# Loads of x blocks 4 to 7 and of the feed-forward weights: from ScalarE's queue to SyncE's, behind a store that waits for block 2

## The chip, the cores and the metric

The kernel runs on one core of a Trainium2 chip. A core has five engines with a queue of instructions each: TensorE (PE, matrix products; its weight loads are listed apart as PEld), VectorE (DVE), ScalarE (ACT), GpSimd (POOL) and SyncE (SP), which here only issues transfers. Transfers run on 16 DMA engines that all queues share. The metric is device time in microseconds of one execution; less is better. Times quoted are the median of three runs, beside which one execution was profiled.

## The reference

The input x has 4 batches of 1024 tokens with 256 features. Four layers follow one another, each with a residual and with a layer norm in front:

```python
x = x + _L0_attn_a_ref(_layernorm(x), ...)   # linear recurrent unit (LRU)
x = x + _L0_ffn_ref(_layernorm(x), ...)      # feed-forward with two top-k gates
x = x + _L0_attn_b_ref(_layernorm(x), ...)   # attention, 8 heads of 64
x = x + _L0_ffn_ref(_layernorm(x), ...)      # the same feed-forward weights again
```

The LRU computes, for each batch, a complex linear recurrence over the tokens, and from its states the output:

```python
u = einsum('btd,edh->ebth', x, W_in) + b_in          # real, imaginary, direct
h[t] = lam * h[t-1] + gamma * (u[0] + i u[1])
out = h.real @ W_mid[0] - h.imag @ W_mid[1] + u[2]   # and b_mid
y = gelu(out @ w1_w + w1_b) @ w2_w + w2_b + out
y = layernorm(y) * ln_g + ln_b
```

The feed-forward layer makes logits by a grouped projection, a batch norm over all 4096 tokens (this is why it needs all blocks before it can go on), a gelu and a product with `lin_w`. It keeps the 32 largest of 256 softmax values on the output side and on the input side, and multiplies with one 256 x 256 weight.

## The kernel before

**Blocks.** x lies in eight SBUF tiles `blocks[0]` to `blocks[7]` of 512 tokens (512 KB each). Block k belongs to batch k // 2; the two blocks of a batch hold its even and its odd tokens (`by_block`), so that one recurrence with 512 steps serves both. Each tile has its own place, so none of the x loads waits for space.

**The LRU stage** (up to about 293 us) works block by block:
- `lru.head(xb[k])` (line 357) normalizes a block: DVE takes the statistics (L133, L134) and the inverse root (L55 to L66, L136), ACT scales (L145, `xn`), PE transposes (L147), ACT rounds the result to `xnt[k][0]` (L160) and DVE forms the remainder `xnt[k][1]` (L161). The transposed blocks have four buffers.
- `lru.states` (line 381) makes the states of one batch for one half c of the features: PE products `pu` (L170), evacuated by ACT into `u` (L390), then the recurrence on DVE (L402 to L416). `lru.evacuated` collects the ACT instructions of L390: numbers 0 to 3 belong to batch 0, 4 to 7 to batch 1.
- `lru.outputs` (line 422) is the way from the states to the new x of a block: PE `po` (L170, L437), ACT `ot` (L438), PE `pz` (L443), ACT gelu `zt` (L446), PE (L452), DVE (L455), PE transposes `py` (L465), statistics on DVE, ACT `yn` (L474), POOL (L482 to L484).

`tile_kernel` writes them down in this order: heads of blocks 0 and 1, states of batch 0, `output_weights`, heads of blocks 2 and 3, states of batch 1; then a loop over k with `lru.outputs` of block k, states of a later batch, `lru.head` of block k + 4, and from k = 2 on `f1.head` of block k - 2, which begins the first feed-forward layer. `f1.head` stores transposed inputs with SP (`tt`, L527).

**Loads.** SP loads blocks 0 and 1 at the start. ACT's queue loads the LRU's weights at the start, blocks 2 and 3 after the first `xnt` cast, `brow` (the gain and base rows) after `evacuated[3]`, and then, after `evacuated[7]`, blocks 4 to 7 and all of `ffn_weights` (line 995): the weight `w.wf`, the logits' weight `lint` in four pieces, and nine rows of 1 KB for the biases. The rows come in three groups: each group clears a tile `v` of a single buffer on POOL (L1028), loads one row into three partitions (L1030), and splits it into three bf16 parts by ACT casts (L1031, L1034, L1036) and POOL subtractions (L1032, L1035). The products that read `lint`, `linb` and `wf` are in the feed-forward layers, from 293 us on.

**What sets the order.** A planner orders each engine's instructions when the program is built, by their place in the source and by its own estimate of when their inputs are there; afterwards an engine takes its instructions strictly in that order, and each waits for what it needs. `with tc.issue_after(ins):` puts the instructions that the block writes on the engine of `ins` behind `ins` in that engine's order; it puts no order on other engines. In `with tc.issue_after(lru.evacuated[7])` it holds ACT's DMA issues and ACT's casts.

Of the kernel before, what the change touches and what calls it, by code (L numbers as in the profile page):

```python
# [10 lines left out]
F32 = mybir.dt.float32  # L11
# [10 lines left out]
P = 128  # L22
B = 4
T = 1024
D = 256
# [3 lines left out]
NBLK = B * T // 512  # L29
# [143 lines left out]
def by_block(v):  # L173

    return [
        v[b * T : (b + 1) * T, :].rearrange("(q p r) d -> r p q d", p=P, r=CH)[r] for b in range(B) for r in range(CH)
    ]
# [807 lines left out]
def run(*gens):  # L985
    for g in gens:
        for _ in g:
            pass
# [6 lines left out]
def ffn_weights(nc, rp, cp, w, lint, lin_t, w_ffn, rows):  # L995
    vecs = w.vecs


    grp = cp.tile([P, 32], F32, tag="grp", name="grp")
    nc.gpsimd.memset(grp, 1.0)  # L1000
    nc.gpsimd.affine_select(
        out=grp, in_=grp, compare_op=ALU.is_ge, fill=0.0, base=0, pattern=[[-4, 32]], channel_multiplier=1
    )
    nc.gpsimd.affine_select(
        out=grp, in_=grp, compare_op=ALU.is_ge, fill=0.0, base=3, pattern=[[4, 32]], channel_multiplier=-1
    )
    for s in range(2):
        for k in range(KD):
            nc.gpsimd.tensor_scalar(
                w.cw[:, k, s * 32 : (s + 1) * 32],  # L1010
                grp,
                vecs[:, V_CW + 2 * s + k : V_CW + 2 * s + k + 1],
                0.0,
                ALU.mult,
                ALU.add,
            )
    nc.gpsimd.memset(lint, 0.0)
    for s in range(2):
        for k in range(KD):
            r = k * 64 + s * 32  # L1020
            nc.scalar.dma_start(lint[r : r + 32, s, :], lin_t[s, k * 32 : (k + 1) * 32, :])
    nc.scalar.dma_start(w.wf, w_ffn)

    nc.gpsimd.memset(w.ones, 1.0)
    parts = [slice(32 * i, 32 * i + 32) for i in range(3)]
    for dst, at in ((w.linb[:, 0:D], 0), (w.linb[:, D : 2 * D], D), (w.bias, 4 * D)):
        v = rp.tile([P, D], F32, tag="v", name="v")
        nc.gpsimd.memset(v, 0.0)  # L1028
        for i in range(3):
            nc.scalar.dma_start(v[32 * i : 32 * i + 1, :], rows[0:1, at : at + D])  # L1030
        nc.scalar.copy(dst, v)  # L1031
        nc.gpsimd.tensor_tensor(v, v, dst, ALU.subtract)  # L1032
        for i in (1, 2):
            nc.scalar.copy(dst[parts[i], :], v[parts[i], :])  # L1034
        nc.gpsimd.tensor_tensor(v[parts[2], :], v[parts[2], :], dst[parts[2], :], ALU.subtract)  # L1035
        nc.scalar.copy(dst[parts[2], :], v[parts[2], :])  # L1036
# [3 lines left out]
def tile_kernel(ctx: ExitStack, tc: tile.TileContext, x_in, w_lru, vecs_in, rows, w_ffn, lin_t, w_attn, w_down, out):  # L1040
    nc = tc.nc
# [9 lines left out]
    def load_x(engine, blk):  # L1051
        engine.dma_start(blocks[blk], by_block(x_in)[blk])
# [9 lines left out]
    w = Weights()  # L1062
    w.ident, w.vecs = ident, vecs
    w.wf = cp.tile([P, KD, D], F32, tag="wf", name="wf")
    lint = cp.tile([P, 2, D], F32, tag="lint", name="lint")
# [5 lines left out]
    f1 = Ffn("f1", tc, bp, x, w)  # L1071
# [3 lines left out]
    with ExitStack() as c1:  # L1075
        psum = Banks(c1.enter_context(tc.tile_pool(name="ps1", space=PSUM)), {"pu": 2, "po": 2, "py": 2, "pt": 2})

        brow = c1.enter_context(tc.tile_pool(name="brow", bufs=1)).tile([P, 2, D], F32, tag="brow", name="brow")
        lru = Lru(tc, c1, ident, vecs, brow, w_lru, psum)
        xb = [x[4 * k : 4 * k + 4] for k in range(NBLK)]  # L1080
        xnt = [lru.head(xb[0])]
        lru.tables(lambda: xnt.append(lru.head(xb[1])))
        with tc.issue_after(lru.xnt_first):
            for blk in range(2, 4):
                load_x(nc.scalar, blk)
        h = [[lru.states(xnt, c) for c in range(KD)]]
        lru.output_weights()
        with tc.issue_after(lru.evacuated[3]):
            nc.scalar.dma_start(brow.rearrange("p a b -> p (a b)"), rows[0, 2 * D : 4 * D].partition_broadcast(P))
        xnt += [lru.head(xb[k]) for k in (2, 3)]  # L1090
        h.append([lru.states(xnt[2:4], c) for c in range(KD)])
        for k in range(NBLK):
            last = k >= NBLK - 2
            if k == 0:
                with tc.issue_after(lru.evacuated[7]):
                    for blk in range(4, NBLK):
                        load_x(nc.scalar, blk)
                    ffn_weights(
                        nc, c1.enter_context(tc.tile_pool(name="rows", bufs=1)), cp, w, lint, lin_t, w_ffn, rows
                    )  # L1100
            if k < NBLK - 1:
                run(lru.outputs(k % CH, xb[k], xnt[k], h[k // CH], (0, 1), last))

            b = k // CH + 1
            if 2 <= b < B:
                if k % CH == 0:
                    h.append([])
                h[b].append(lru.states(xnt[b * CH : (b + 1) * CH], k % CH))
            if k + 4 < NBLK:
                xnt.append(lru.head(xb[k + 4]))  # L1110
            if 2 <= k < NBLK - 2:
                run(f1.head(k - 2, lru.sp, psum, "pt"))
        for blk in range(4, NBLK - 3):
            run(f1.head(blk, lru.sp, psum, "pt"))
        k = NBLK - 1
        ot, zt = lru.buffers()
        halves = [
            lru.outputs(k % CH, xb[k], xnt[k], h[k // CH], (i,), last, tag, [v[:, :, c : c + 256] for v in (ot, zt)])
            for i, tag, c in ((0, "pu", 0), (1, "po", 256))
        ]  # L1120
        for i in (0, 0, 1):
            next(halves[i])
        run(f1.head(NBLK - 3, lru.sp, psum, "pt"))
        for i in (0, 1, 0, 1, 0, 1, 1):
            next(halves[i])
        with tc.issue_after(lru.last_gelu):
            run(f1.head(NBLK - 2, lru.sp, psum, "pt"))
        run(*(f1.head(NBLK - 1, lru.sp, psum, "pu", (i,), "lx", "zt") for i in range(2)))

    with ExitStack() as c2:  # L1130
# [7 lines left out]
        at = Attention(tc, x, ident, ident64, wqk, wvo, wd, sp, wp)  # L1138
        with ExitStack() as c4:
# [14 lines left out]
            first = at.prepare(0, 0, psum, "at")  # L1154
# [170 lines left out]
```

## Time and profile before

| | us |
|---|---|
| median of 3 runs | 1529.46 (1526.32 to 1533.48) |
| profiled execution, its own time | 1528.76 |
| profiled execution, span | 1527.0 |
| busy PE, DVE, ACT, POOL | 1286.5, 1184.6, 1017.5, 680.3 |

All times in the profile count from the start of the span. The timelines give the start and the length of instructions in order of time, those of one kind that follow one another merged (x4 means four of them); an engine's name with a q, such as ACTq, is its queue issuing a transfer. In brackets stands how long the engine sat idle before the instruction, and whose end let it go. The lists of waits give the total, the number and the longest. The LRU stage fills the first fifth of the span, the first feed-forward layer follows until about 390 us, attention with the second layer's heads between until about 1310, and the rest is the second feed-forward layer.

Over the span the page has 96.51 MB moved, a mean of 63 GB/s.

### The profile page before, as it was taken

To read this page: it belongs to the slowest core of one execution; us is meant where nothing else is said; L and a number is where in the kernel's file an instruction comes from. 1 tells how busy PE (TensorE), PEld (TensorE's weight loads), DVE (VectorE), ACT (ScalarE), POOL (GpSimd) and SP (SyncE) were. 2 spreads that over 40 slices of the span, in tenths; PEclk is the share of its full clock that TensorE was granted. 3 is DMA by queue.
4 is the path that set the end of the run, shared out by engine and by line. 5 is a ranking of instruction groups with operands and counts; after the bars stand their busy time and mean duration, and the time that the engine had idled before them with its cause. 6 is when DMAs were issued, how large, how long until landed. Compare 5 with 4: busy or idle time off the path is not lost. (4 is left out here: it accounts for less than half of the span.)

```text
span 1527.0 us, 28727 instructions
## 1 busy us (share of the span) xinstructions
PE 1286.5 (84%) x10134; PEld 955.6 (63%) x10136; DVE 1184.6 (78%) x3682; ACT 1017.5 (67%) x2152; POOL 680.3 (45%) x849
## 2 busy tenths in 40 slices
PE   4879998697898898888998989889999999566675
PEld 3535465376677766766776767677777777334454
DVE  8976665697868887878768687777676675599998
ACT  5353433566887877797777787877777776475674
POOL 2033332161545454544544554454344444067776
PEclk9999999698999999999999999999999999688899
DMA  3110000321454343434433445334344545000000
GB/s 118 32 41 15 21 21 21 128 97 49 84 93 90 61 77 73 77 70 82 82 74 60 72 79 86 61 61 83 68 82 79 92 86 96 1 15 24 22 25 28
DMA packets 288609, 96.51 MB, mean 63 GB/s; under 512 B 268233, under 2 KB 284626, under 8 KB 288466
## 3 DMA queue, kind: packets, MB, share of 16 engines
q1 hardware_dynamic: 283024, 88.50, 28.7%
q10 hardware_dynamic: 5442, 6.18, 1.2%
q8 instruction: 80, 1.31, 0.4%
q14 instruction: 63, 0.52, 0.1%
HBM read 16.01 MB, written 11.53 MB: 18 GB/s over the span
## 5 line engine op out<-in xcount | busy, mean ns | idle before, releaser
L898 POOL TENSOR_TENSOR pd<-pr,pd 128x1024 f16<-128x1024 f32 x128 | 273.5, 2141 | 247.6 <-ACT pd L897 185.7
L890 DVE TENSOR_REDUCE nm<-sc 128x1 f32<-128x1024 f32 x256 | 308.5, 1217 | 78.9 <-PE sc L886 77.5
L894 ACT ACTIVATE pr<-sc,nm 128x1024 f32<-128x1024 f32 x256 | 285.9, 1119 | 84.6 <-DVE nm L892 47.0
L886 PE MATMUL sc<-kh,qs 128*128 128x512 f32 x512 | 184.3, 438 | 26.4 <-ACT pr L894 18.8
L886 PE MATMUL sc<-kl,qs 128*128 128x512 f32 x512 | 162.0, 397 | 0.0
L674 DVE MATCH_REPLACE8 wk<-m,wk 128x256 f32<-128x256 f32 x384 | 154.9, 406 | 0.1
L910 ACT COPY p<-ptp 128x512 f32<-128x512 f32 x224 | 124.1, 590 | 45.3 <-PE ptp L905 33.7
L674 DVE MAX8 m<-wk 128x8 f32<-128x256 f32 x384 | 151.3, 412 | 0.4
L930 PE MATMUL pmo<-p,la 128*64 128x128 f32 x2048 | 144.0, 289 | 6.1 <-ACT ft L524 2.9
L905 PE MATMUL ptp<-ident,pr 128*128 128x128 f32 x1024 | 138.3, 275 | 12.9 <-ACT pr L894 12.4
L930 PEld LDWEIGHTS pmo<-p,la 128*64 128x64 f32 x2048 | 122.8, 144 | 25.0 <-ACT ft L524 5.1
L905 PEld LDWEIGHTS ptp<-ident,pr 128*128 128x128 f32 x1024 | 115.6, 140 | 34.8 <-ACT pr L894 22.2
L897 ACT CAST pd<-pr 128x1024 f16<-128x1024 f32 x128 | 133.5, 1054 | 5.6 <-DMA d<-pd 4.6
L886 PEld LDWEIGHTS sc<-kh,qs 128*128 128x128 f32 x512 | 85.2, 195 | 51.1 <-ACT pr L894 29.8
L886 PEld LDWEIGHTS sc<-kl,qs 128*128 128x128 f32 x512 | 97.0, 190 | 23.2 <-issue 1.4
L930 PE MATMUL pmo<-d,lb 128*64 128x128 f16 x3072 | 103.4, 222 | 7.6 <-DVE qs L853 2.6
L930 PEld LDWEIGHTS <-lb 128*64 128x64 f16 x3072 | 92.2, 111 | 26.3 <-issue 20.1
L628 POOL TENSOR_TENSOR ex<-ex,wk 128x512 f32<-128x512 f32 x61 | 77.6, 1273 | 57.4 <-DVE wk L674 45.5
L926 POOL COPY rows<-rs 128x128 f32<-128x128 f32 x128 | 36.1, 294 | 124.4 <-PE pmo L938 76.3
L941 DVE TENSOR_TENSOR on<-pmo,rb 128x128 f32<-128x128 f32 x128 | 36.4, 285 | 66.8 <-ACT rb L940 66.3
L147 PE MATMUL pt<-ident,xn 128*128 128x128 f32 x256 | 47.8, 309 | 44.5 <-ACT xn L145 32.9
L699 PE MATMUL pf<-wf,vt 128*128 128x256 f32 x288 | 81.2, 427 | 4.6 <-ACT vt L697 4.2
(307 smaller groups left out, 2768.6 us busy)
## 6 DMA issues: line engine op xcount, KB each, us to landing
tt<-ft SPq DMA_DIRECT2D x16, 256.0 KB
tt<-tt SPq DMA_DIRECT2D x8, 512.0 KB
out<-x SPq DMA_DIRECT2D x32, 128.0 KB
x<-in_x ACTq DMA_DIRECT2D x6, 512.0 KB
pf<-pfs SPq DMA_DIRECT2D x12, 256.0 KB
full<-pf SPq DMA_DIRECT2D x24, 128.0 KB
d<-pd SPq DMA_TRANSPOSE x128
wa<-in_w_attn SPq DMA_DIRECT2D x2, 640.0 KB
```

Source lines behind the costliest of these rows:

```text
L147: nc.tensor.transpose(pt[:, k, i * P : (i + 1) * P], xn[:, k * P : (k + 1) * P], ident)
L628: pool.tensor_tensor(ex, ex, wk, ALU.subtract)
L674: ins = make(*args).ins
L699: nc.tensor.matmul(dst, vt[:, k, :], w.wf[:, k, :], start=(k == 0 and bias is None), stop=(k == KD - 1))
L886: nc.tensor.matmul(sc[:, sl], qs[:, j, q * P : (q + 1) * P], kk[:, sl], start=(i == 0), stop=(i == 1))
L890: nc.vector.tensor_reduce(nm, sc, AX.X, ALU.max, negate=True)
L894: nc.scalar.activation(pr, sc, AF.Exp, bias=nm, accum_out=ssum[:, j : j + 1])
L897: nc.scalar.copy(pd[:, 0, :], pr)
L898: nc.gpsimd.tensor_tensor(pd[:, 1, :], pr, pd[:, 0, :], ALU.subtract)
L905: nc.tensor.transpose(pt[:, kk, :], pr[:, kc * P : (kc + 1) * P], self.ident)
L910: nc.scalar.copy(dst, pt)
L930: nc.tensor.matmul(po[j * HD : (j + 1) * HD, 0, :], v, pts[j][:, c, :], start=(n == 0), stop=(n == len(terms) - 1),)
```

## The change

Two things change. The loads of `lint`, `wf` and the nine `v` rows are issued by SP in place of ACT, and so are the loads of blocks 4 to 7. And their place in the order is given by a new instruction: SP stores one column of `xnt[2][0]` (128 partitions, 4 bytes each) to a scratch tile `gate` in DRAM, which nothing reads; the loads stand behind it on SP. The store waits for the data that it reads, which ACT's cast writes in the head of block 2; the loads behind it wait with it. In the source the x loads now stand ahead of the states of batch 1, and `ffn_weights` stays where it was.

```diff
@@ ffn_weights
-            nc.scalar.dma_start(lint[r : r + 32, s, :], lin_t[s, k * 32 : (k + 1) * 32, :])
-    nc.scalar.dma_start(w.wf, w_ffn)
+            nc.sync.dma_start(lint[r : r + 32, s, :], lin_t[s, k * 32 : (k + 1) * 32, :])
+    nc.sync.dma_start(w.wf, w_ffn)
...
-            nc.scalar.dma_start(v[32 * i : 32 * i + 1, :], rows[0:1, at : at + D])
+            nc.sync.dma_start(v[32 * i : 32 * i + 1, :], rows[0:1, at : at + D])
@@ tile_kernel
         xnt += [lru.head(xb[k]) for k in (2, 3)]
+        gate = f1.dram.tile([P, 1], F32, tag="gate", name="gate")
+        first = nc.sync.dma_start(gate, xnt[2][0][:, 0, 0:1].bitcast(F32)).ins
+        with tc.issue_after(first):
+            for blk in range(4, NBLK):
+                load_x(nc.sync, blk)
         h.append([lru.states(xnt[2:4], c) for c in range(KD)])
         for k in range(NBLK):
             last = k >= NBLK - 2
             if k == 0:
-                with tc.issue_after(lru.evacuated[7]):
-                    for blk in range(4, NBLK):
-                        load_x(nc.scalar, blk)
+                with tc.issue_after(first):
                     ffn_weights(
                         nc, c1.enter_context(tc.tile_pool(name="rows", bufs=1)), cp, w, lint, lin_t, w_ffn, rows
                     )
```

## The prediction

> **What bounds the kernel now.** I read the waits of each engine first, cut to the first 400 us, because every moved instruction lies there; then the timelines of ScalarE (ACT) and TensorE (PE) around the moved loads; then windows of 1 us, and wider ones after them, to see who is the limit before and behind that place. The longest waits that touch a moved load are one of ACT and, behind it, one of PE:
>
> ```profile
> ACT ot L438 <- DMA wf<-in_w_ffn: 9.2, 1, 9.2
> PE pz L443 <- ACT ot L438: 8.2, 1, 8.2
> ```
>
> The timeline of ACT shows what the 9.2 us are (start, length, engine, line, what):
>
> ```profile
> 72.19 0.78 ACT L390 ACTIVATE u<-pu,gb,par_o 128x512 f32<-128x512 f32 x1 [2.02 <-DVE h L402]
> 72.20 2.05 ACTq L1052 DMA_DIRECT2D x<-in_x  x4
> 74.29 2.02 ACTq L1021 DMA_DIRECT2D lint<-in_lin_t  x4
> 76.35 0.43 ACTq L1022 DMA_DIRECT2D wf<-in_w_ffn  x1
> 77.16 4.96 ACTq L1030 DMA_DIRECT2D v<-in_rows  x3
> 82.17 1.26 ACT L438 ACTIVATE ot<-po,ob 128x512 f32<-128x512 f32 x2 [9.20 <-DMA wf<-in_w_ffn]
> ...
> 87.25 0.84 ACTq L1030 DMA_DIRECT2D v<-in_rows  x3
> 88.12 1.28 ACT L446 ACT_TABLE_LOAD   x1 [1.28 <-DMA v<-in_rows]
> ```
>
> And that of PE, what stood behind it:
>
> ```profile
> 72.00 2.74 PE L437 MATMUL po<-h,wm 128*128 128x512 f32 x6
> 82.91 5.17 PE L443 MATMUL pz<-ot,w_lru 128*128 128x512 f32 x8 [8.18 <-ACT ot L438]
> 90.15 3.70 PE L452 MATMUL pz<-zt,w_lru 128*128 128x512 f32 x8 [2.08 <-ACT zt L446]
> ...
> 105.11 1.88 PE L443 MATMUL pz<-ot,w_lru 128*128 128x512 f32 x4
> ```
>
> The reader is to see that `po` of block 0 was finished at 74.74 and that ACT could not evacuate it before 82.17, because twelve DMA issues stood ahead of it in its queue. Three windows tell who is the limit (width, then busy us of PE, PE's weight loads, DVE, ACT, POOL; PE clock, DMA share, GB/s):
>
> ```profile
> 40.00:60.00 20.00, 15.75 (x67) 11.93 (x66) 20.00 (x33) 7.37 (x14) 0.00 (x0) 0.91 0.05 13
> 79.00:80.00 1.00, 0.00 (x0) 0.00 (x0) 1.00 (x5) 0.00 (x0) 0.00 (x0) 0.54 1.09 383
> 130.00:160.00 30.00, 29.36 (x107) 16.50 (x105) 22.08 (x59) 13.40 (x25) 13.18 (x22) 1.00 0.05 18
> 160.00:200.00 40.00, 36.99 (x133) 21.83 (x134) 25.27 (x76) 15.99 (x29) 16.36 (x24) 0.96 0.08 27
> ```
>
> VectorE (DVE) is never idle from 20 to 90 us; from about 95 to 240 us PE is the limit (92 to 98% busy). The stall lies at the joint: PE has work for blocks 0 and 1 at 75 us that needs no further states, and loses 8 us. So microseconds given to PE at 75 should survive: PE is short of time until 240, the stage behind it (240 to 290) is a chain of dependent steps, and the feed-forward layer cannot start its batch norm before all blocks are through.
>
> **What is removed.** ACT loses 4 x loads (2.05 us), 4 `lint` loads (2.02), `wf` (0.43) and nine `v` rows. The first three `v` take until 82.12: the second starts at 79.9 and the third at 81.9, though one issue lasts 0.23 to 0.47. Meanwhile the DMA engines are full (share 1.00 to 1.09 in most microseconds from 74 to 81), so the queue held the issuer back. The sum on PE:
> - The gap of 8.18. Without the DMAs, ACT evacuates `po` at 74.8; one evacuation (0.7 us) of the second half stays in the way: gain 7.5.
> - The clock. In the gap PE's granted clock falls to 0.54 and stays at 0.50 until 85; the eight L443 took 5.17 where four take 1.88 later, so 3.76: gain 1.4.
> - The second gap of 2.08: the activation table (1.28) is loaded at 88.12, behind casts and three more issues (0.84). The first half of `pz` would be finished 1.9 us after L443 starts, and table plus activation (1.28 + 0.63) then lie beside the other half: gain 1.8.
> - The third group of issues (0.84 at 94.4) delayed an `xnt` cast by 0.6, with PE busy: nothing.
> Together 10.7 us.
>
> Here a rule speaks against so much. The Trainium skill, "DMA: Bandwidth & Descriptors", section "Issuing engines are not separate DMA queues", says that choosing another issuing engine saves only the time to initiate a DMA, usually small beside the transfer, since all share the same 16 engines. By the rule only the issues count: 2.05 + 2.02 + 0.43 + 0.47 + 2 x 0.23 = 5.4 us from 72.97, so ACT would have been free at 78.4 and PE loses only 78.4 - 74.7 = 3.7; with the second gap that makes 5.5. The row says free at 82.17. I take the row: the issuer is blocked by the full queue as well, and after the change nothing urgent stands behind it. The bandwidth, as the rule has it, does not improve.
>
> **What is added and moved.** SP gets one store of 128 x 4 bytes. It waits for the `xnt` cast of block 2: 40.87 + 0.58 = 41.45 for its first half, or 47.7 if the whole tile counts. Behind it on SP come the 18 loads, in order; then nothing until the first `tt` store at 134.38. SP was empty from 2 to 134 us, so issue time there costs nothing. No row shows a store so small; bounds are 0 and the 3.5 us that x4 needed from issue (72.2) to first use (75.75). Nobody waits for its landing and x is not needed before 75: 0.
>
> The transfers, 2.5 MB, took from 73 to 81.6 and would run from 42 to 51 (or 48 to 57). The DMA share is 0.00 from 40 to 46; then only `brow` runs, first read at 105. Cost 0.
>
> The nine casts on ACT (0.40 each, 3.6 us) and POOL's three memsets and six subtractions come earlier. A group took 5.8 to 7.2 us from its first cast to that of the next (83.33, 90.57, 96.39), so three end about 72. ACT has idle stretches of 7.57, 1.78 and 6.31 us between 52 and 69, POOL is empty there: cover exists. Without cover, a cast that stands in ACT's queue ahead of its landing holds the `u` evacuations; DVE reaches block 2's `u` at 61.77, and it was ready at 60.5, so only 1.3 us of slack. POOL also disturbs DVE: beside POOL's subtraction at 83.80 DVE's L56 took 0.63 instead of 0.16. Six subtractions of 0.66 to 0.94 are 4.3 us, so this costs between 0 and 4.3; I take 1, as DVE's large operations (0.66 to 0.68) were not lengthened beside it.
>
> x4 to x7 in place by 51: their layer norms need about 18 us of DVE, now at 75 to 116 us. Done earlier in small holes they would help: a PE gap of 3.03 at 113.65 waited for DVE's L455, behind block 7's statistics. Put ahead of the state recurrences they would hurt. Bounds -3 and +18; I take 0, as both `lru.states` calls are written before those heads.
>
> **Sum**: -10.7 + 1 = -9.7. The profiled execution took 1528.76 us (span 1527.0 and 1.8 around it), which gives 1519; the median of the three runs is 1529.46, which gives 1520. I say 1520.0.
>
> **Rivals.**
> - *The wait moves to the casts.* The queue orders are fixed beforehand by a planner's own estimate of landings. If it places the first `linb` cast before block 3's `xn` at 46.67, ACT waits for the row behind 2.5 MB, until 51.5: 5 us, of which 1.3 is slack; with all of POOL's 4.3 on DVE it gives back 8. Result -10.7 + 8, about 1527. For it: DVE has no slack there. Against it: after 15 us ACT's only waits for a landing in this trace are of 0.8 us or less, apart from the queue's hold above.
> - *DVE's order turns.* With x4 to x7 early, the statistics (16 of 0.40, 16 of 0.15, and four inverse roots of a dozen operations each, 0.15 to 0.65) slip into the recurrences of batches 0 and 1. PE's L437 at 62.1 needs those states. Up to 18 us pushed ahead of it, less the 9.7: 1538. It decides once more than 9.7 us of statistics stand before the last L415 (61.17) on DVE. For it: DVE is the limit there, and 8 of those 18 us lay between the recurrences already at 75 to 90. Against it: their data order puts them behind, and the norm's buffers are double only.
> - *The change doesn't act*: `po` is not evacuated at 74.8 because something else stands ahead (the `linb` casts of group 3, or the planner puts L438 elsewhere): 0, about 1529. Small, as the DMAs are gone from ACT in any case; I count it with the first rival.
>
> **Chances.** Forecast 0.52 (own range 1514 to 1525); casts or no effect 0.23 (1523 to 1532); DVE's order, or another queue order that costs, 0.25 (1533 to 1545). A measurement of this kernel tells about 0.5% (7.6 us; the three runs lie 7.2 apart) from no change. Of the forecast's 0.52, 0.42 lies below 1521.8; the rest and the first rival make 0.33; slower is 0.25. The range 1513 to 1540 leaves out the fast end and the far part of the last case.
>
> **What would show it.** Right: on ACT no DMA issue after 20 us but `brow`; L438 within 1 us of the end of L437 near 75; PE's clock stays at 1.0 from 74 to 86; L446's table load directly behind L443's first half; the end of the LRU stage (293.4, first `wf` cast) about 10 us earlier. Wrong: an ACT wait for `v` between 45 and 70; layer-norm statistics of x4 to x7 before 61 on DVE and L437 later than 62; or the 10 us gained at 90 gone by 290, which would mean that PE was not the limit between.

## The result: slower by 0.6%, and the profile after

The changed kernel takes 1538.29 us (median of 9 runs, 1530.63 to 1545.40), the kernel before in the same comparison 1528.68 (9 runs, 1524.52 to 1533.48): ratio 1.0062, 95% interval 1.0037 to 1.0086. The forecast was 1520. The profiled execution after has a span of 1535.6 us.

I read the waits of the first 400 us first, as before (total, number, longest). In the kernel after they show two new waits, both for x, and the pair of waits at `ot` and `pz` is no longer among the longest:

```profile
DVE lx_st L133 <- DMA x<-in_x: 12.8, 3, 7.3
...
ACT xnt L160 <- DMA x<-in_x: 7.4, 1, 7.4
...
ACT linb L1031 <- DMA v<-in_rows: 5.0, 2, 2.8
```

The timelines of the same kernel, of SP, DVE, ACT and PE in turn, give the place:

```profile
41.84 0.34 SPq L1093 DMA_DIRECT2D gate<-xnt  x1
42.23 2.07 SPq L1052 DMA_DIRECT2D x<-in_x  x4
44.41 9.42 SPq L1021 DMA_DIRECT2D lint<-in_lin_t  x4
55.67 0.35 SPq L1022 DMA_DIRECT2D wf<-in_w_ffn  x1
...
45.63 1.22 DVE L410 TENSOR_TENSOR_SCAN h<-rad,h 128x512 f32<-128x512 f32 x1
54.17 1.08 DVE L133 BATCH_NORM_STATS2 lx_st<-x 128x6 f32<-128x256 f32 x3 [7.32 <-DMA x<-in_x]
...
54.17 0.35 ACTq L1089 DMA_DIRECT2D brow<-in_rows  x1
54.55 0.59 ACT L160 CAST xnt<-pt 128x512 fp32r<-128x512 f32 x1 [7.43 <-DMA x<-in_x]
...
82.48 0.69 ACT L438 ACTIVATE ot<-po,ob 128x512 f32<-128x512 f32 x1 [0.94 <-PE po L437]
...
71.54 3.60 PE L437 MATMUL po<-h,wm 128*128 128x512 f32 x8
84.00 3.60 PE L443 MATMUL pz<-ot,w_lru 128*128 128x512 f32 x8
```

The store is issued at 41.84 and the four x loads right behind it, as foreseen. But block 4 lands only at about 54, 12 us after its issue. The planner has put block 4's statistics (L133) right behind the first recurrence of batch 0 (L410) on DVE, the engine that this stage waits for, and DVE stands still for 7.3 us. In the kernel before, these statistics came behind batch 0's states, and `po` earlier (timelines of DVE and PE):

```profile
75.75 1.08 DVE L133 BATCH_NORM_STATS2 lx_st<-x 128x6 f32<-128x256 f32 x3
...
62.11 4.45 PE L437 MATMUL po<-h,wm 128*128 128x512 f32 x10
```

ACT stands too: the issue of `brow` (L1089) is released by the same landing, and the `xnt` cast of block 3 is queued behind it. PE's `po` products start at 71.54 where they started at 62.11, and `ot` comes at 82.48, no earlier than before (82.17), though no DMA issue stands in its way any more.

Windows of 1 us of the kernel after, and the 20 us that were shown of before (columns as there), tell why x was late:

```profile
43.00:44.00 1.00, 1.00 (x6) 0.82 (x5) 1.00 (x3) 0.39 (x1) 0.00 (x0) 1.00 0.25 49
44.00:45.00 1.00, 1.00 (x6) 0.77 (x6) 1.00 (x2) 0.39 (x1) 0.00 (x0) 1.00 0.00 0
...
47.00:48.00 1.00, 1.00 (x7) 0.82 (x6) 0.00 (x0) 0.12 (x1) 0.00 (x0) 1.00 0.42 22
...
50.00:51.00 1.00, 0.00 (x0) 0.00 (x0) 0.00 (x0) 0.00 (x0) 0.00 (x0) 1.00 0.52 27
...
52.00:53.00 1.00, 0.00 (x0) 0.00 (x0) 0.00 (x0) 0.00 (x0) 0.00 (x0) 1.00 0.96 311
...
40.00:60.00 20.00, 11.35 (x53) 8.72 (x54) 12.68 (x27) 7.02 (x13) 0.00 (x0) 0.86 0.59 137
```

Between 44 and 52 the queue moves 0 to 100 GB/s, with 2 MB of loads issued; then it runs at 311 GB/s and more. DVE, 20.00 of 20 us busy before, is busy for 12.68.

What became of the loss, from the same points in both profiles (us; the last column is `g_pitch`, the kernel with the spread-out store, explained below):

| point | before | after | after, spread store |
|---|---|---|---|
| imaginary part of batch 0's states finished (DVE L416) | 61.25 | 74.99 | 67.81 |
| real part finished (DVE L415); now all of them are there | 61.85 | 77.44 | 70.25 |
| first `ot` (ACT L438) | 82.17 | 82.48 | 76.14 |
| last step of the first batch norm (DVE L548, end of the LRU stage) | 296.82 | 299.31 | 287.79 |
| first row maximum of attention (DVE L890) | 378.15 | 384.18 | 372.93 |
| last step of the second batch norm (DVE L548) | 1325.13 | 1334.36 | 1325.96 |
| span | 1527.0 | 1535.6 | 1527.2 |

15.6 us are lost at batch 0's states (13.7 at the imaginary part, which is the point that the expectations below give). By the end of the stage 13 of them are made good; the stall at 75 is gone. Then 3.5 more are lost before attention, and the remaining 3.2 to the second batch norm.

### The profile page after: what moved, and what is told of

Its sections match the earlier page's. It is cut to its first block, busy times and chain, and to the rows that moved or that the text cites. A ratio compares the mean times of both kernels' runs of the same rounds, so it can differ in the third digit from the quotient of the medians.

```text
span 1535.6 us, 28749 instructions
## 1 busy us (share of the span) xinstructions
PE 1296.9 (84%) x10136; PEld 960.9 (63%) x10136; DVE 1179.1 (77%) x3682; ACT 1019.4 (66%) x2152; POOL 684.7 (45%) x849
## 5 line engine op out<-in xcount | busy, mean ns | idle before, releaser
L890 DVE TENSOR_REDUCE nm<-sc 128x1 f32<-128x1024 f32 x256 | 308.9, 1219 | 82.4 <-PE sc L886 81.0
L894 ACT ACTIVATE pr<-sc,nm 128x1024 f32<-128x1024 f32 x256 | 286.1, 1120 | 82.9 <-DVE nm L892 47.9
L674 DVE MATCH_REPLACE8 wk<-m,wk 128x256 f32<-128x256 f32 x384 | 160.7, 426 | 0.1
L674 DVE MAX8 m<-wk 128x8 f32<-128x256 f32 x384 | 155.5, 431 | 0.4
```

The costliest lines, as they stand in the source:

```text
L674: ins = make(*args).ins
L890: nc.vector.tensor_reduce(nm, sc, AX.X, ALU.max, negate=True)
L894: nc.scalar.activation(pr, sc, AF.Exp, bias=nm, accum_out=ssum[:, j : j + 1])
```

## Experiments

Theory A: the 128 four-byte writes of the store hold up the loads behind them in the queue, and x comes late for DVE. Theory B: the early place of the loads costs, by the planner's order (statistics of x4 to x7 and `v` casts ahead of the recurrences), or by transfers beside the work. All edits are made to the changed kernel.

**A wide store** (`wide`): 512 bytes for each partition in place of 4. Every queue has the same order.

```diff
-        gate = f1.dram.tile([P, 1], F32, tag="gate", name="gate")
-        first = nc.sync.dma_start(gate, xnt[2][0][:, 0, 0:1].bitcast(F32)).ins
+        gate = f1.dram.tile([P, P], F32, tag="gate", name="gate")
+        first = nc.sync.dma_start(gate, xnt[2][0][:, 0, 0:P].bitcast(F32)).ins
```

> The store ahead of the loads writes rows of 512 bytes (128 x 128 values) instead of 4 bytes; every engine's order of instructions is that of the changed kernel. Theory A (x4's data came 8 us late because they crept behind 128 writes of 4 bytes): the transfers of x4 to x7 start at about 43 and run at 300 GB/s or more, DVE's wait of 7.3 us for x4 and ACT's of 7.4 us shrink below 2, the states of batch 0 end near 68 instead of 75, and the time falls by 4 to 8 us, to 1530 to 1534. Rival B (the loads are slow there for another reason, or the wait is off the path): the wait stays at about 7 us, or it goes and the time stays at 1536 to 1540.

1533.80 us (14 runs), ratio to before 1.0019 (1.0003 to 1.0036). The store moves 128 times as much and the loads behind it run at 221 GB/s from 43 us; DVE does not wait for x4; states of batch 0 finish at 69.78 (the imaginary part at 67.33), first `ot` at 74.82. The stall belongs to the small store, not to the place of the loads. But of the 15.6 us lost at batch 0's states 7.9 stay, and the time is not below before's.

**Each half of the loads alone** (`xonly`, `wonly`): behind the four-byte store only the x loads, or only the weights and rows; the others go back to ACT behind `evacuated[7]`.

```diff
# xonly: lint, wf and v
-nc.sync.dma_start(
+nc.scalar.dma_start(
-                with tc.issue_after(first):
+                with tc.issue_after(lru.evacuated[7]):
                     ffn_weights(
# wonly: x
-        with tc.issue_after(first):
-            for blk in range(4, NBLK):
-                load_x(nc.sync, blk)
...
+                with tc.issue_after(lru.evacuated[7]):
+                    for blk in range(4, NBLK):
+                        load_x(nc.scalar, blk)
```

> Only the x loads go to SP behind the 4-byte store; lint, wf and the rows stay on ACT after evacuated[7]. Theory A (x4's early statistics and their late data are the loss): DVE still waits about 7 us for x4 near 47 and the time is that of the changed kernel or a little above, 1535 to 1542. Rival C (the rows' casts on ACT between 60 and 78 are the loss, since they hold the evacuations of u): without them 1526 to 1531.

1540.15 us, ratio 1.0063 (1.0045 to 1.0081): the whole loss, with the DVE wait of 7.2 us.

> Only lint, wf and the rows go to SP behind the 4-byte store; x blocks 4 to 7 stay on ACT after evacuated[7], so DVE's order up to the states of batch 1 is that of before. Theory A: no wait for x4 before 72, ACT issues four loads (2.05 us) and evacuates po at about 75, PE's gap of 8.2 us falls to 1, and the sum of the prediction shows: 1519 to 1524. Rival C (the casts hold the evacuations of u): states of batch 0 later than 64 and 1528 to 1538. Rival D (PE is not the limit between 95 and 290, so what is won at 75 is lost again): the first evacuation of po is 7 us earlier, and the feed-forward layer starts less than 3 us earlier, 1526 to 1530.

1527.49 us, ratio 0.9984 (0.9971 to 0.9996). The transfers behind the store crawl here as well (61, 70, 13, 12 GB/s in the microseconds from 44 to 48), but nobody waits for `lint` or `wf`. So the slow queue costs time only through x. Theory A's time (1519 to 1524) was missed: the first `ot` comes at 76.70 and the stage ends 3.9 us ahead of the kernel before's, but the time is only about 2.5 us lower.

**The same loads behind a later store** (`late`): the store reads the first half of batch 1's states, at about 72 us, in rows of 512 bytes.

```diff
+        h.append([lru.states(xnt[2:4], 0)])
+        gate = f1.dram.tile([P, P], F32, tag="gate", name="gate")
+        first = nc.sync.dma_start(gate, h[1][0][1][:, 1 : 1 + P]).ins
...
-        h.append([lru.states(xnt[2:4], c) for c in range(KD)])
+        h[1].append(lru.states(xnt[2:4], 1))
```

> All loads go to SP as in the change, but the store ahead of them has rows of 512 bytes and reads the states of batch 1's first half, so it leaves near 72 us, where the loads stood before. Theory A: DVE's order keeps the statistics of x4 behind the recurrences, no wait above 2 us for x4, and the gain of the prediction shows: 1517 to 1523. Rival D (the gain is lost again before the feed-forward layer): 1526 to 1531. Rival E (another order of the later stages costs by itself, whatever the first 100 us do): over 1531 although the first evacuation of po comes 6 us or more before 82.

1526.02 us, ratio 0.9984 (0.9969 to 0.9998). States of batch 0 finish at 62.10, first `ot` 74.40, the LRU stage ends 7.2 us before that of the kernel before. Most of the forecast's gain is there; at the end only about 2.5 us are left of it. The time is that of rival D, but the loss lies behind the place that D named.

**What makes the small store slow** (`g_64`, `g_pitch`): 64 bytes for each partition; and the same 128 writes of 4 bytes, but 512 bytes apart in DRAM. In both every queue has the changed kernel's order.

```diff
# g_64
+        gate = f1.dram.tile([P, 16], F32, tag="gate", name="gate")
+        first = nc.sync.dma_start(gate, xnt[2][0][:, 0, 0:16].bitcast(F32)).ins
# g_pitch
+        gate = f1.dram.tile([P, P], F32, tag="gate", name="gate")
+        first = nc.sync.dma_start(gate[:, 0:1], xnt[2][0][:, 0, 0:1].bitcast(F32)).ins
```

> The changed kernel with a store of 128 rows of 64 bytes; the order on all engines is the same but for SP's waits. If what stalls the loads is the number of small writes to few bytes of DRAM, rows of 64 bytes stall them less: x4 between 46 and 51. If any row below 512 bytes stalls them as 4 bytes do: x4 at 54, DVE's wait 7 us. If 4 bytes alone do: x4 by 47 and no wait.

> The changed kernel with the same 128 writes of 4 bytes, but 512 bytes apart in DRAM instead of side by side. If the writes stall the loads because they fall on the same few bytes of DRAM one after another: x4 by 47 and DVE's wait below 2 us. If 4-byte rows are slow wherever they go: x4 at 54 and a wait of 7 us.

One run each: 1522.49 and 1529.00 us. Neither has the DVE wait, and the transfers run at 266 and 331 GB/s in the microsecond from 44. So writes of 4 bytes are not slow as such; 128 of them side by side, in 512 bytes of DRAM in all, are.

`g_pitch` was then timed, beside the changed kernel on the same chip (`again`, `pitch5`; `pitch5` is `g_pitch` once more).

> The changed kernel once more, as the partner of the run with spread-out store addresses, on the same chip. Both theories: 1538 us, ratio to before about 1.006 (1.0037 to 1.0086 so far); DVE again waits about 7 us for x behind the first states of batch 0, and the transfers behind the store stay near 0 to 34 GB/s from 44 to 52 us.

> The changed kernel with the 128 writes of the store 512 bytes apart in DRAM, timed; nothing else differs on any queue. If the loss is the DVE wait behind 128 adjacent writes: no DVE wait for x, first ot near 76, batch norm 8 to 9 us earlier than in the changed kernel, and a median of 1529 to 1533, ratio to before 0.999 to 1.002. If the early place of the loads, or their queue, is what costs: as the changed kernel, 1536 to 1540, ratio above 1.004.

1541.01 us (6 runs, ratio 1.0083, 1.0059 to 1.0108) against 1530.28 (22 runs, ratio 1.0014, 1.0003 to 1.0025): 10.7 us from the DRAM addresses of a store that nobody reads. Windows of `pitch5`, columns as above:

```profile
43.00:44.00 1.00, 1.00 (x6) 0.82 (x5) 1.00 (x2) 0.78 (x1) 0.00 (x0) 1.00 0.81 239
44.00:45.00 1.00, 1.00 (x6) 0.80 (x5) 1.00 (x3) 0.00 (x0) 0.00 (x0) 1.00 1.08 352
...
50.00:51.00 1.00, 0.00 (x0) 0.00 (x0) 1.00 (x5) 1.00 (x3) 0.00 (x0) 1.00 1.05 309
...
52.00:53.00 1.00, 0.14 (x2) 0.00 (x0) 1.00 (x3) 0.04 (x1) 0.00 (x0) 1.00 0.05 16
...
40.00:60.00 20.00, 14.26 (x60) 10.76 (x59) 20.00 (x45) 9.00 (x18) 2.88 (x3) 0.83 0.44 138
```

The loads run from 43 to 52, and DVE is busy for all of the 20 us. The timelines of `pitch5`, of DVE, ACT and PE:

```profile
45.21 1.22 DVE L410 TENSOR_TENSOR_SCAN h<-rad,h 128x512 f32<-128x512 f32 x1
46.34 1.05 DVE L133 BATCH_NORM_STATS2 lx_st<-x 128x6 f32<-128x256 f32 x3
...
76.11 0.69 ACT L438 ACTIVATE ot<-po,ob 128x512 f32<-128x512 f32 x1 [0.94 <-PE po L437]
...
82.39 0.93 PE L147 MATMUL pt<-ident,xn 128*128 128x128 f32 x4 [1.17 <-ACT xn L145]
84.89 6.54 PE L452 MATMUL pz<-zt,w_lru 128*128 128x512 f32 x8 [1.56 <-ACT zt L446]
```

L133 stands in the same place behind L410, and finds its data there.

The traces also show when the store itself was done. All of its 4-byte pieces are recorded by 42.88 us in the kernel after. Each transfer leaves 16 completion marks in the trace. Those of the store come between 45.77 and 50.02 in the kernel after (45.66 to 49.77 in `again`), but all between 42.65 and 42.85 in `pitch5` and between 43.22 and 43.42 in `g_64`. Meanwhile single pieces of the loads, 1 KB each and 0.046 us in the median, took up to 5.2 us; in `pitch5` the longest took 0.73. The list of transfers of `wonly` gives the store's time from issue to landing (KB, us):

```profile
gate<-xnt SPq DMA_DIRECT2D x1, 0.5 KB, 8.1
```

So it is the store itself that lands late, and the loads behind it come up to speed only after its last mark (in `again` too: 49.77, and 359 GB/s from 52).

**The early statistics held back** (`wide_heads`): the wide store, and the heads of blocks 4 to 7 behind the recurrences of batch 1 on DVE.

```diff
-                xnt.append(lru.head(xb[k + 4]))
+                with tc.issue_after(lru.scanned[3]):
+                    xnt.append(lru.head(xb[k + 4]))
```

> The wide store with the early loads, but DVE's part of the heads of blocks 4 to 7 may only be issued behind the last instruction of batch 1's states. Theory H (early statistics between the recurrences cost DVE time even when the data are there): states of batch 0 end near 62 to 65 instead of 67.3, those of batch 1 near 84 to 88 instead of 93.3, the batch norm comes 1 to 3 us earlier than with the wide store alone, and the time is 1527 to 1532. Rival D (DVE's order there is off the path, because PE has other work): the states come earlier and the batch norm does not, 1532 to 1535.

1530.86 us, ratio 0.9986 (0.9967 to 1.0005). In the profile of the changed kernel 28 operations of these statistics, 8.2 us of DVE, stand between 45.5 us and the end of batch 0's states; here none does, and the states finish at 63.01 in place of 69.78. The first `ot` moves only from 74.82 to 74.55, the batch norm by 2.3 us. Timelines of ACT and PE in `wide_heads`:

```profile
76.97 1.28 ACT L446 ACT_TABLE_LOAD   x1
...
76.06 3.60 PE L443 MATMUL pz<-ot,w_lru 128*128 128x512 f32 x8
79.58 3.70 PE L452 MATMUL pz<-zt,w_lru 128*128 128x512 f32 x8
```

This is the joint as the forecast drew it: the table load beside L443, no gap ahead of L452.

**Where the gain of the stage goes** (`late_gelu`, `best`, `before_b`). The way from the first batch norm to the first row maximum of attention takes 81.3 us before, 81.8 in `wide_heads` and 83.5 to 85.7 in every other profile of this study's kernels. Lines of `late`, of PE and ACT in that stage:

```profile
346.07 3.78 PE L567 MATMUL pfa<-wf,tt 128*128 128x256 f32 x8 [3.95 <-ACT ob L650]
...
339.81 4.34 ACT L587 ACTIVATE xc_f<-xc_f,bt,bs 128x512 f32<-128x512 f32 x6
344.16 1.28 ACT L155 ACT_TABLE_LOAD   x1
345.56 0.46 ACT L650 ACTIVATE ob<-pf,rs 128x256 f32<-128x256 f32 x1
```

And in the kernel before:

```profile
349.34 1.99 PE L567 MATMUL pfa<-wf,tt 128*128 128x256 f32 x8 [2.04 <-ACT ob L650]
...
348.84 0.45 ACT L650 ACTIVATE ob<-pf,rs 128x256 f32<-128x256 f32 x1
349.19 0.80 ACT L587 ACTIVATE xc_f<-xc_f,bt,bs 128x512 f32<-128x512 f32 x1
```

The planner now puts all six gelus (L587) and a table load ahead of tile 5's output (L650); before, the output stood ahead of the sixth. PE waits 3.95 us in place of 2.04, and its next eight products take 3.78 in place of 1.99: PE's granted clock, as a share of full speed, is 0.50 there (346 to 350 in `late`) and 1.00 in the kernel before (349 to 352). `late_gelu` is `late` with the last gelu and the table load written behind that output:

```diff
-                        for blk in range(2, NBLK):
-                            g = f1.gelu(blk)
-                    with tc.issue_after(g):
-                        warm(nc, sp, AF.Exp)
+                        for blk in range(2, NBLK - 1):
+                            f1.gelu(blk)
...
+                if i + 2 == TPB:
+                    with tc.issue_after(f1.obs[-2]):
+                        g = f1.gelu(NBLK - 1)
+                    with tc.issue_after(g):
+                        warm(nc, sp, AF.Exp)
```

> The kernel with the late wide store, and in the first feed-forward stage the last of the six gelus is put behind the evacuation ob of tile 5 on ACT (L650 in the kernel before), the order that the kernel before has there. Theory F (the 3.2 us lost between the batch norm and the first scores are this one swap: PE waits 4.0 instead of 2.0 us and then runs eight products in 3.8 instead of 2.0 us): that stage falls from 84.6 to about 81.5 us, the same as before, and the time by 2 to 4 us against the late store alone, to 1520 to 1524. Rival G (the loss is spread over many small differences of order): the stage stays above 84 and the time at 1525 to 1528.

```profile
341.99 1.99 PE L567 MATMUL pfa<-wf,tt 128*128 128x256 f32 x8 [1.75 <-ACT ob L650]
...
337.94 3.63 ACT L587 ACTIVATE xc_f<-xc_f,bt,bs 128x512 f32<-128x512 f32 x5
341.48 0.45 ACT L650 ACTIVATE ob<-pf,rs 128x256 f32<-128x256 f32 x1
```

More than half of the wait and the slow products are gone. The last tile of that layer is finished 5.0 us earlier than in `late`, of which 2.1 were there at the stage's start, so the order is worth 2.9; 1.1 of these are left at the first row maximum (370.98, 7.2 ahead of the kernel before). So the stage takes 83.5 us, and not the 81.5 of theory F. The whole takes 1528.26 us, ratio 0.9979 (0.9965 to 0.9993), hardly more than `late` gained by its ratio: in this profile attention takes 4.0 us more than in that of `late`.

> 64-byte rows in the store, the heads of blocks 4 to 7 behind the recurrences of batch 1 on DVE, and the last gelu with its table load behind tile 5's output as in the kernel before. If the stage's gain holds once neither the store nor the early statistics nor the order of the gelus gives it back: batch norm 7 to 9 us earlier than before, first scores 7 to 10 us earlier, median 1519 to 1523, ratio 0.993 to 0.997. If the later stages take back what the first gives whatever their order (because PE or DVE is near its limit there): 1527 to 1531, ratio 0.998 to 1.001.

`best` joins the 64-byte store, the heads of `wide_heads` and the gelus of `late_gelu`: 1530.65 us (21 runs), ratio 1.0014 (1.0003 to 1.0025). The second reading held. At the batch norm it is 8.25 us ahead of before's profile, at the first row maximum 5.69, at the end level. No version that was timed more than once is faster by 0.5%.

> The kernel before, profiled a second time, for the length of its later stages. In the first profile it took 81.33 us from the batch norm to the first scores and 946.98 from there to the second batch norm; the six kernels with the changed order (as changed, and with wider or spread-out stores) took 83.5 to 85.7 and 946.5 to 958.8, mean 953.3. If the changed order itself gives the gain back there: again about 81.3 and 945 to 950. If it is scatter between executions: 81 to 86 and anything up to 959.

80.26 and 945.24 us, as in the first reading. From the batch norm to the first row maximum the changed order takes 84.1 to 85.7 in its six profiles (the changed kernel's, `again`, `wide`, `g_64`, `g_pitch`, `pitch5`), before's 80.3 and 81.3. In attention one more loss repeats: from the 25th to the 31st row maximum 23.6 to 23.8 us in all six, 21.5 and 21.6 before. There ACT's order differs (an exponential, L894, stands ahead of the cast of `qs`, L852, for which PE waits); that place was not tried alone, and `late` and `wide_heads` do not have the loss (21.6 and 21.5). The rest of attention scatters between profiles of one and the same order by more than the question: 946.5 to 958.8.

This scatter goes with PE's granted clock. In the six profiles of the changed order attention is the longer, the longer the clock stood at 0.50 in it: 51 us in the shortest (`g_64`), 80 in the longest (`wide`). The timed runs agree: 0.01 less in a run's mean clock goes with about 7 us more among the 22 runs of `pitch5`, whose mean clock is 0.939 against 0.944 for the kernel before in the same comparison (`best` 0.941; `late` 0.941 against 0.943 in its own). By that slope, as an estimate, 3.7 us of what `pitch5` does not keep go with the clock. Whether the new order lowers the clock, or waits lower it and the clock only shows them, no run here separates.

## Why the prediction failed, step by step

**The stall and its removal: right in place and size, wrong in the cause.** `ot` was to come at 74.8 and came at 74.40 (`late`) and 74.55 (`wide_heads`); that is a gain of 7.8 us against the kernel before, where the rule, by issue times alone, allowed 3.7 (ACT free at 78.4, measured 82.17). The eight L443 were to take 3.76 and took 3.60. The gap behind them goes in `wide_heads`, and is still there, in two parts, in `pitch5` (1.17 and 1.56), where ACT scales a block ahead of the table load. But ACT was not held by a full queue. In the program that was built, transfers share eight completion counters in turn, and one whose counter is still in use waits for the earlier transfer's landing. ACT's list in the kernel before reads:

```
L1022 DMACopy wf<-in_w_ffn 128x512 [waits DMAHW4_49]
L1030 DMACopy v<-in_rows 1x256 [waits DMAHW5_49]
L1030 DMACopy v<-in_rows 1x256 [waits DMAHW6_49]
L1030 DMACopy v<-in_rows 1x256 [waits DMAHW7_49]
```

Counted in turn, these four counters are those of x blocks 4 to 7, and the third row waits for block 7. The trace agrees: blocks 5, 6 and 7 are complete at 77.14, 79.92 and 81.87, and the three rows are issued at 77.16, 79.94 and 81.89. In the kernel after, `brow` waits for DMAHW4, again that of block 4. This is why the issue on ACT stood until 54.17 for loads that SP had issued. An issue can be held as well: in the kernel after, where the loads ahead of it crawled, SP's first `lint` issue took 7.97 us, in `pitch5` 0.45. In the kernel before none of these loads took longer than 0.60 to issue. The forecast checked SP's queue for what stands behind the wait, not the counters that tie the queues together.

**The transfers: right once the store is out of the way** (43 to 52 in `pitch5`, predicted 42 to 51).

**The store at nothing: the step that failed.** It was bounded by 0 and 3.5 us, from what a large load took to land, with "Nobody waits for its landing and x is not needed before 75". No product or activation waits for the store (`lint`'s fourth piece shares its counter, which cost nothing); but the loads behind it in the queue came 12 us after their issue, and by the planner's new order DVE needed x from about 47 us on. The two together hang 10.7 us of the kernel's time on the store; without the early x the slow store shows no cost in the time (`wonly`). No row of the trace before showed a small write, and the bound was taken from a large read. The Trainium skill, "DMA: Bandwidth & Descriptors", section "Specifications", says that below 512 bytes a transfer is done by read-modify-write. That rule spoke against the store and was not weighed. It would fit with 128 such writes to the same 512 bytes; yet rows of 64 bytes, and 4 bytes with 512 between them, lie below that size too and did not stall, so the size alone does not decide. That the store's own writes end only between 45.77 and 50.02 the trace shows; why they take so long where they lie side by side stays open.

**The early statistics at 0: wrong reason.** "Both `lru.states` calls are written before those heads" did not hold the planner: 8.2 us of them stand ahead of the end of batch 0's states. With their data in time these states come 7.8 us later (`pitch5` against before), inside the bounds of -3 and +18, and the first `ot` 0.3 to 1.8 later (`wide` and `g_64` against `wide_heads`). At the end of the stage their cost is below the scatter: profiles of the same order without the stall end it at 287.8 to 292.0. This is the rival "DVE's order turns": its time, 1538, came true and its place too, but not its price; that the number fits is luck. The work in front stayed under its own point of 9.7 us, and alone gives `pitch5`; the slow side was a wait for data, which the rival did not name.

**The casts at 1.** Not separated. The sign that was named for them, an ACT wait for `v` between 45 and 70, came (5.0 us in two waits in the kernel after), but what it cost no run isolates. In `wide_heads`, where casts and rows are early and statistics are not, batch 0's states finish 1.2 us later than before; in `wonly`, behind the slow store, 3.3.

**"Microseconds given to PE at 75 survive": true to the end of the stage, not to the end of the kernel.** Without the stall the eight profiles that have the gain (`wide`, `g_64`, `g_pitch`, `pitch5`, `late`, `late_gelu`, `wide_heads`, `best`) end the stage 4.8 to 9.3 us ahead of 296.82, where 9.7 were forecast. The sum was then set against the whole time as though the later stages kept their length. The signs that it named for this step lay before 290; the gain went behind that, about 4 us in the feed-forward layer (an order of ACT is behind 2.9 of them at the layer's last tile, by `late_gelu`) and 2.2 at one place of attention in the changed order (read off, not tried); some of the rest goes with the clock. So even without the store's stall the changed order would have been within 0.5% of before.

## What to carry to other kernels

A transfer that is used only as a marker is still work in its queue: give it rows of the size that other transfers there have, or at least addresses apart, and read the rate of the loads behind it. Data that arrive early are only a gain if no engine's fixed order starts to rely on them; look for what a planner pulls forward, and which other queue shares a completion counter with them. And a gain inside one stage is a claim about that stage: where a planner orders everything behind it anew, check the length of each later stage before adding it to the end.

## What was not expected of the hardware

- 128 writes of 4 bytes to 512 consecutive bytes of DRAM held the loads behind them in the queue to 0 to 100 GB/s for 8 us (44 to 52); the same writes 512 bytes apart let them run at 352 GB/s from 44 (`pitch5`). The store took 0.34 us to issue and 8.1 to land (`wonly`).
- Placing the store's bytes elsewhere in DRAM was worth more (10.7 us) than what the removal of the 8.18 us stall on PE left at the end (about 2.5 us in `late`).
